# Audio tower on one core: two key blocks read in 64-row matmuls, one expert between the reads, moves on two queues

## The chip, the cores and the metric

The kernel runs on one core of a Trainium2 chip. The time is the device time of one execution in microseconds; lower is better. TensorE is called PE here, VectorE DVE, ScalarE ACT, GpSimd POOL and SyncE SP, as in the profile.

## What is computed

All arithmetic is in fp32. 64 audio signals of 80,000 samples are padded and cut into 157 frames of 512, and each frame goes through a 512-point cosine transform: `h` of 64 x 157 x 512. Then come an attention layer without a softmax and a layer with 16 experts, each behind a layer norm and with a residual.

```python
key_phase = jnp.tanh(x @ Wk + bk) * pi          # 4 sets of 8 planes
query_phase = jnp.tanh(x @ Wq + bq) * pi
V = x @ Wv + bv
for s in range(N_SETS):                          # causal: cumsum over time
    bound = key_ph[:, :, s, :, None] * V[:, :, None, :]
    memory = jnp.cumsum(bound, axis=1)
    retrieved = (memory * jnp.conj(qry_ph[:, :, s, :, None])).sum(axis=2).real
    total = total + weights[s] * retrieved
...                                              # the same once more with fixed phases of the position
total = gate * total + (1.0 - gate) * pos_contrib
return x + total / norm @ Wo + bo
...
scores = softmax(mean(x, axis=1) @ Wg + bg);  idx = argmax(scores)
y = einsum('bsd,bdo->bso', x, We[idx]) + be[idx];  out = scores[idx] * y
```

The running sums are written as a masked product: every query sums the values of all keys not later than itself, weighted with the cosine of the phase difference.

## The kernel before

The 64 examples are worked in 16 groups of 4 (`GB`). A group's tokens are cut into 5 blocks of 32 per example: tile `n` holds one block of each of the 4 examples, 4 x 32 = 128 rows. Tiles 0 to 3 and `TAIL` = 4 hold the time blocks 1, 2, 3, 0 and 4 (`BLOCK`); in the free axis tokens stand in the order `SLOT`.

The order of the work is written out by hand, function by function, and each engine runs its own instructions in that order. Group `g` goes through these stages; the experts of group `g - 1` and the cosine transform of group `g + 1` are set in between:

- `project_and_values(g)`: key and query projections (L600), the values by seven half-size products in place of eight (`value_product`, L445) and the tail's values by a plain product (L250). The values of tiles 0 to 3 lie in two buffers of tag `v`, the tail's in one of tag `v_t`. In between, the normalized tokens of `g - 1` are transposed in blocks of 32x32 by DVE (`turn_blocks`, L780) into a buffer with the tag `gT`. `move_blocks` (L782 to L790) issues 16 DMAs on SP that move them between partitions into `x2T`, which the experts read. After it `route` and `pick` choose each example's expert, and `fetch` (L890) gathers four weight matrices by indirect DMA from POOL.
- `gate(g)`: seven gate products (`gate_product`, L655), whose first copy out of PSUM (L462) writes a new buffer of tag `gT`, so it waits until the moves have read the old one. After the product with `i == 5`, `scores(g)` (L674 to L683) makes the weights `att` of all key blocks: per tile and example a matmul of keys by queries, 32 columns of the array each, into one bank, then two DVE operations. `SEES` says which slots of the queries a key tile is seen by; all tiles side by side are `NS` = 480 columns, with the mask `hmask`.
- `experts_and_embedding(g)`: the experts of `g - 1` for the tail and for tiles 0 and 1 (`expert`, L936, sets of four matmuls that take 32 columns of the array each), the transform of `g + 1` (L270, L272) and its statistics; ACT copies its results out of PSUM (L292, L293) and, after POOL's deviations, scales the residuals (L323).
- `attention(g)`: `read(g, c)` for the four chunks `c` of 128 output features. A read is 20 matmuls of 32 rows (L697): for each key tile one per example, from the array's four row groups into four banks, with 320, 256, 192, 128 and 64 columns for the tiles 3, 0, 1, 2 and `TAIL` (half for the learned phases, half for the fixed ones). A bank pair is one PSUM buffer, and there are four of these; a read takes two. DVE combines each read with the gate in four operations (L705). Then the expert of tile 2 of `g - 1`, and the output products (`output_product`, L445, and the tail's L250), with the expert of tile 3 inside.

Groups 0 and 15 have no expert of an older group between or behind the reads. Group 0 has its own beginning (`first_values`, `first_gate`), and after group 15 come the last experts.

Of the kernel before, what the change touches and what calls it, by code (L numbers as in the profile page):

```python
# [14 lines left out]
F32 = mybir.dt.float32  # L15
# [5 lines left out]
B, L, D = 64, 157, 512  # L21
T_IN = 80000
P = 128
C = D // P
H = D // 2
GB = 4
NG = B // GB
LP = 160
Q = P // GB
NM = LP // Q  # L30
TAIL = NM - 1
SLOT = [0, 1, 3, 4, 2]
# [6 lines left out]
E = 16  # L39
# [3 lines left out]

SEES = [(0, 4 * Q), (Q, 4 * Q), (2 * Q, 4 * Q), (0, LP), (2 * Q, 3 * Q)]
START = [sum(hi - lo for lo, hi in SEES[:n]) for n in range(NM)]
NS = sum(hi - lo for lo, hi in SEES)

# [4 lines left out]
def audio_tower(ctx: ExitStack, tc: tile.TileContext, a, out):  # L54
# [420 lines left out]
    def value_buffer(g, n):  # L475

        s = S[g]
        if n == TAIL:
            s["v", n] = p1.tile([P, D], F32, tag="v_t", name="v_t")
        else:  # L480
            s["v2", n // 2] = v = p1.tile([P, 2, D], F32, tag="v", name="v", bufs=2)
            for b in range(2):
                s["v", n + b] = v[:, b, :]
# [19 lines left out]
    def keep_product(g):  # L503

        s = S[g]
        i, ps = s.pop("ps")
        if i == 1:
            value_buffer(g, 0)
            value_buffer(g, 2)
        gather(i, ps, [[s["v2", m][:, :, n : n + H] for n in (0, H)] for m in range(2)])  # L510

    def add_bv(g, m, of=slice(0, D)):
        v = S[g]["v2", m][:, :, of]
# [17 lines left out]
    def constants():  # L531


        nc.vector.tensor_scalar(hbg, hbg, 0.5, None, ALU.mult)

        sw = lambda name, n: small.tile([2 * F, n], F32, tag=name, name=name, bufs=1)
        mx, ex, sm, rs, pk = sw("sw1", 1), sw("sw2", SETS), sw("sw3", 1), sw("sw4", 1), sw("sw5", 1)
        nc.vector.tensor_reduce(mx, setw, AX.X, ALU.max)
        nc.vector.tensor_scalar(ex, setw, mx, None, ALU.subtract)
        nc.scalar.activation(ex, ex, AF.Exp)  # L540

        nc.scalar.activation(sigp, posw, AF.Tanh, scale=0.5)

        turns = p2.tile([2 * PLANES, LP], F32, tag="even", name="turns")
        nc.vector.tensor_scalar(turns, pos, freqs, None, ALU.mult)
        for _ in range(2):
            whole = p2.tile([2 * PLANES, LP], F32, tag="be", name="whole", bufs=1)
            nc.vector.tensor_scalar(whole, turns, ROUND, ROUND, ALU.add, ALU.subtract)
            rest = p2.tile([2 * PLANES, LP], F32, tag="even", name="rest")
            nc.vector.tensor_tensor(rest, turns, whole, ALU.subtract)  # L550
            turns = rest
        folded = p2.tile([2 * PLANES, LP], F32, tag="be", name="folded", bufs=1)
        nc.vector.scalar_tensor_tensor(folded, turns, ptrig[:, 0:1], turns, ALU.mult, ALU.max)
        nc.scalar.activation(pf, folded.rearrange("p (s t) -> p s t", t=Q), AF.Sin, bias=ptrig[:, 2:3], scale=ptrig[:, 1:2])
        nc.gpsimd.memset(kf[2 * F :], 0.0)
        nc.gpsimd.memset(qf[2 * F :], 0.0)
        yield
        nc.vector.tensor_reduce(sm, ex, AX.X, ALU.add)
        nc.vector.reciprocal(rs, sm)
        nc.vector.tensor_tensor(ex, ex, setsel, ALU.mult)  # L560
        nc.vector.tensor_reduce(pk, ex, AX.X, ALU.add)
        nc.vector.tensor_tensor(wvec, pk, rs, ALU.mult)
        nc.vector.tensor_scalar(sigp2, sigp, 1.0, None, ALU.add)
        nc.vector.tensor_scalar(sigp, sigp, 0.5, 0.5, ALU.mult, ALU.add)
        yield
        ps = bank()
        for n in range(NM):
            lo, hi = SEES[n]
            for i in range(GB):
                to = ps[Q * i : Q * (i + 1), START[n] : START[n] + hi - lo]  # L570
                nc.tensor.matmul(to, pf[:, SLOT[n]], pf[:, lo // Q : hi // Q], start=True, stop=True)
        nc.vector.scalar_tensor_tensor(share, ps[:, :NS], sigp2, hmask, ALU.mult, ALU.mult)
        yield
        rows = slice(2 * F, 2 * F + 2 * PLANES)
        for i in range(GB):
            nc.gpsimd.tensor_copy(kf[rows, :, i], pf)
            nc.vector.tensor_scalar(qf[rows, :, i], pf, sigp[: 2 * PLANES], -1.0, ALU.mult, ALU.mult)
        yield
# [95 lines left out]
    def scores(g):  # L674

        ps = bank()
        for n in range(NM):
            lo, hi = SEES[n]
            for i in range(GB):
                to = ps[Q * i : Q * (i + 1), START[n] : START[n] + hi - lo]  # L680
                nc.tensor.matmul(to, kf[:, SLOT[n], i], qf[:, lo // Q : hi // Q, i], start=True, stop=True)  # L681
        nc.vector.tensor_tensor(att[:, 0], ps[:, :NS], hmask, ALU.mult)
        nc.vector.tensor_tensor(att[:, 1], att[:, 0], share, ALU.add)  # L683

    def read(g, c):

        s = S[g]
        parts = [psum(), psum()]
        banks = [ps[:, b, : 2 * LP] for ps in parts for b in range(2)]

        for n in (3, 0, 1, 2, TAIL):
            for i in range(GB):
                q = slice(Q * i, Q * (i + 1))
                lo, hi = SEES[n]
                to = banks[i].rearrange("p (s t) -> p s t", s=2)[:, :, lo:hi]
                by = att[q, :, START[n] : START[n] + hi - lo]
                nc.tensor.matmul(  # L697
                    to, s["v", n][q, c * P : (c + 1) * P], by, start=(n == 3), stop=(n == TAIL)
                )
        for k, ps in enumerate(parts):  # L700
            of = slice(2 * k, 2 * k + 2)
            r = ps[:, :, : 2 * LP].rearrange("p b (s n t) -> p b s n t", s=2, n=NM)
            th = s["gT"][:, c].rearrange("p (n b t) -> p b n t", n=NM, b=GB)[:, of]
            for n, op in enumerate((ALU.mult, ALU.add)):
                nc.vector.tensor_tensor(th, r[:, :, n], th, op)  # L705
# [76 lines left out]
    def move_blocks(g):  # L782

        s = S[g]
        x = p1.tile([P, GB, C, LP], F32, tag="x2T", name="x2T")
        of = s["blocks2"].rearrange("p (q c) t -> p q c t", c=C)
        for b in range(GB):
            for q in range(GB):
                nc.sync.dma_start(out=x[Q * q : Q * (q + 1), b], in_=of[Q * b : Q * (b + 1), q])  # L789
        s["x2T"] = x.rearrange("p b c t -> p c b t")  # L790

    def turn_x2(g, n, copy=nc.scalar.copy):
        s = S[g]
# [20 lines left out]
    def route_own(g):  # L814

        s = S[g]
        late, total = s.pop("late"), s.pop("early")
        add(total, total, late)
        part = p2.tile([P, E, C * GB], F32, tag="u", name="part")
        nc.vector.tensor_tensor(part, rwq, total.unsqueeze(1).to_broadcast([P, E, C * GB]), ALU.mult)  # L820
        each = p2.tile([P, E], F32, tag="each", name="each")
        nc.vector.tensor_reduce(each, part, AX.X, ALU.add)
        own = p2.tile([P, GB, E], F32, tag="own", name="own")
        nc.vector.tensor_tensor(own, quad, each.unsqueeze(1).to_broadcast([P, GB, E]), ALU.mult)
        s["own"] = own.rearrange("p b e -> p (b e)")

# [34 lines left out]
    def pick(g):  # L861
# [5 lines left out]
        s["top"] = top = t("top", [P, GB])  # L867
        nc.vector.tensor_reduce(top, logit, AX.X, ALU.max)

        score = t("score", wide)  # L870
        nc.vector.tensor_tensor(score, logit, over(top), ALU.is_equal)
        nc.vector.tensor_tensor(score, score, revexp, ALU.mult)
        s["rev"] = rev = t("rev", [P, GB])
# [172 lines left out]
    def first_gate():  # L1046
# [13 lines left out]
        scores(0)  # L1060
        embed(1, 2)
        embed_statistics(1, 2)
        for n in (1, 2, 3, TAIL):
            add_bo(0, n)
        weights()
# [15 lines left out]
    def project_and_values(g):  # L1081
# [16 lines left out]
        turn_blocks(g - 1, 0)  # L1098
        keep_value(g, TAIL)
        turn_blocks(g - 1, 1)  # L1100
        move_blocks(g - 1)
        S[g - 1]["late"] = xsum(g - 1, 2 * Q, L)
        value_product(g, 2)
        keep_product(g)
        add_bv(g, 0, slice(0, H))
        phasors(g)
        value_product(g, 6)
        keep_product(g)
# [18 lines left out]
    def gate(g):  # L1127
        ahead = g + 1 < NG
        for i in (1, 6, 2, 7, 5, 4, 3):
            gate_product(g, i)  # L1130
            if i == 1:
# [2 lines left out]
                fold_once(g + 1, 1)  # L1134
                add_bv(g, 0, slice(H, D))
                add_bv(g, 1)
            elif i == 5:
                scores(g)
                fold_twice(g + 1, 1)
                if ahead:  # L1140
# [8 lines left out]
    def experts_and_embedding(g):  # L1149
# [3 lines left out]
        for n in (2, 3, TAIL):  # L1153
            embed(new, n)
            embed_statistics(new, n)
        embed_deviations(new)
        load_half(g + 2, 0)
        load_half(g + 2, 1)
# [9 lines left out]
    def attention(g):  # L1168
# [6 lines left out]
                pass  # L1175
        for c in range(C):
            read(g, c)
        if ahead and g > 0:
            expert(g - 1, 2)
        S[g]["blocks"] = halves(S[g]["gT"])  # L1180
        made = token_sums(g, tail=False)
        if g == 0:
# [93 lines left out]
def _constants():  # L1276
# [15 lines left out]
    def trig(half, n, turn):  # L1292
# [6 lines left out]
    norm = 1.0 / np.sqrt(np.float64(PLANES) * (at + 1))  # L1299
    causal = (np.arange(LP)[:, None] <= at[None, :]) * norm[None, :] * (at < L)[None, :]  # L1300
    causal[L:] = 0.0
    masks = [causal[Q * BLOCK[n] : Q * (BLOCK[n] + 1), lo:hi] for n, (lo, hi) in enumerate(SEES)]
    setsel = np.tile(np.repeat(np.eye(SETS), PLANES, axis=0), (2, 1))
    f = lambda x: np.ascontiguousarray(x, dtype=np.float32)

# [7 lines left out]
        "lift": f(np.concatenate([np.tan(angle), -np.sin(angle) * np.cos(angle)], axis=1)),  # L1313
        "ptrig": trig(PLANES, 1, 2 * PI),
        "pos": f(np.tile(at, (2 * PLANES, 1))),
        "hmask": f(0.5 * np.tile(np.concatenate(masks, axis=1), (GB, 1))),
        "setsel": f(setsel),
        "quad": f(np.repeat(np.kron(np.eye(GB), np.ones((Q, 1)))[:, :, None], E, axis=2)),
        "revexp": f(np.tile(E - np.arange(E), (P, GB, 1))),
# [65 lines left out]
```

## Time and profile before

| What | Value |
|---|---|
| median of 3 runs | 1331.53 us (1330.65 to 1331.94) |
| the profiled execution, its own time | 1333.84 us |
| its span, first to last instruction | 1332.0 us |
| granted TensorE clock over the span | 1.000 |
| busy: PE, DVE, POOL, ACT | 99%, 78%, 42%, 30% |
| the reads' matmuls, L697 | 2560 records, a group's four reads 7.82 us |
| DVE behind the reads, L705 | 256 operations, 116.7 us, 487 ns each |
| SP's moves into x2T, L789 | 240 issues, median 589 ns each |

An fp32 matmul has two records, so a read of 20 matmuls has 40. The ends of matmuls are modelled, and matmuls of different row or column groups overlap; a stretch of PE is therefore best measured from its start to the start of the next stretch. In the timeline a row is a run of instructions of one line, engine and tile, with start, length, what, and in brackets the engine's idle time before it and what ended that; a line that is called the chain gives start, length and what. In the table of waits a line gives who waited for whom, total us, how often, and the longest.

### The profile page before, as it was taken

How to read it: one execution, taken by the hardware profiler on the slowest of the kernel's cores; microseconds unless marked ns; L12 is line 12 of the kernel's file. 1: busy time of each engine (PE TensorE's matmuls, PEld its weight loads, DVE VectorE, ACT ScalarE, POOL GpSimd, SP SyncE). 2: the span in 40 equal slices, each digit the busy share in tenths (PEclk: the TensorE clock that was granted, in tenths of full speed). 3: DMA queues.
4: the chain of work that ended last, by engine and by line, in shares of the span. 5: the costliest groups of instructions: out<-in, count | busy, mean ns of one | idle time of the engine just before them, and what ended most of it. 6: DMA issues, size and time to landing. Idle time of an engine off the chain costs nothing.

```text
span 1332.0 us, 25132 instructions
## 1 busy us (share of the span) xinstructions
PE 1322.8 (99%) x9784; PEld 871.4 (65%) x9784; DVE 1038.9 (78%) x2074; ACT 403.1 (30%) x708; POOL 556.4 (42%) x658
## 2 busy tenths in 40 slices
PE   9999999999999999999999999999999999999998
PEld 6677666675766667576676666757666675766762
DVE  6888788787777878878787787878878788777583
ACT  2524233141333314233142331413333142341410
POOL 2355344344433355244443443344334542444214
PEclk9999999999999999999999999999999999999999
DMA  7015225052341524315153250524415252241506
GB/s 236 1 51 174 82 58 195 19 176 80 115 140 33 177 70 162 93 45 192 35 175 82 69 183 20 177 79 120 136 36 170 74 171 85 46 152 34 177 8 206
DMA packets 62014, 144.40 MB, mean 108 GB/s; under 512 B 14136, under 2 KB 31432, under 8 KB 53960
## 3 DMA queue, kind: packets, MB, share of 16 engines
q1 hardware_dynamic: 49940, 70.06, 19.9%
q0 software_dynamic: 11456, 72.10, 14.1%
q8 instruction: 78, 1.28, 0.4%
q10 hardware_dynamic: 500, 0.64, 0.2%
q14 instruction: 40, 0.33, 0.1%
HBM read 102.47 MB, written 20.62 MB: 92 GB/s over the span
## 4 chain that ended last, share of the span: by engine, by line
PE 94%; SPq 3%; DMA 1%; issue 1%; POOL 1%; ACT 0%; DVE 0%; ACTq 0%; POOLq 0%
PE mm L445 26%; PE mm L936 20%; PE mm L655 16%; PE mm L697 9%; PE mm L250 9%; PE mm L270 3%; SPq L789 3%; PE mm L600 3%; PE mm L272 3%; PE mm L636 1%; PE mm L681 1%; PE mm L201 1%; DMA x2T<-turned 1%; DMA t_v<-in_we,rows 1%; PE mm L219 0%
## 5 line engine op out<-in xcount | busy, mean ns | idle before, releaser
L936 PE MATMUL mm<-we,x2T 128*32 128x512 f32 x2400 | 270.5, 595 | 0.0
L936 PEld LDWEIGHTS mm<-we,x2T 128*32 128x32 f32 x2400 | 74.2, 110 | 156.0 <-issue 149.5
L705 DVE TENSOR_TENSOR gT<-mm,gT 128x320 f32<-128x320 f32 x256 | 116.7, 487 | 23.4 <-PE mm L697 18.9
L697 PE MATMUL mm<-att,v 32*128 32x256 f32 (+3 forms) x2048 | 123.5, 359 | 0.0
L697 PEld LDWEIGHTS mm<-att,v 32*128 32x128 f32 x2048 | 105.0, 185 | 22.3 <-POOL shift L243 6.7
L237 POOL TENSOR_SCALAR rstd<-mv 128x2 f32<-128x2 f32 (+1 forms) x50 | 11.8, 236 | 245.0 <-DVE mv L233 244.9
L237 POOL TENSOR_SCALAR dev<-mv 128x5 f32<-128x5 f32 (+1 forms) x20 | 10.5, 525 | 234.1 <-DVE mv L233 233.5
L771 ACT ACTIVATE x<-res,shift,rstd 128x512 f32<-128x512 f32 x61 | 46.4, 807 | 202.7 <-POOL shift L244 190.8
L515 POOL TENSOR_TENSOR v<-v,bv 128x512 f32<-128x512 f32 (+1 forms) x45 | 72.9, 1635 | 71.0 <-ACT v L464 71.0
L672 ACT ACTIVATE gT<-gT,hbg 128x320 f32<-128x320 f32 x90 | 45.7, 554 | 166.6 <-DVE gT L100 166.6
L947 DVE SCALAR_TENSOR_TENSOR res<-mm,gate,res 128x512 f32<-128x512 f32 x64 | 47.9, 748 | 56.6 <-PE mm L936 56.5
L232 DVE BATCH_NORM_STATS2 st<-res 128x6 f32<-128x512 f32 x128 | 87.8, 686 | 3.3
L890 POOL DMA_INDIRECT we<-in_we,rows x60 | 69.1, 1151 | 44.4 <-issue 33.4
L327 POOL TENSOR_TENSOR res<-res,bo 128x512 f32<-128x512 f32 x64 | 80.3, 1285 | 13.1 <-ACT res L323 13.0
L445 PE MATMUL mm<-t_o,sum 128*128 128x256 f32 x384 | 85.5, 379 | 0.0
L122 POOL TENSOR_TENSOR xT<-xT 128x640 f32<-128x640 f32 x30 | 46.4, 1546 | 88.6 <-DVE even L100 87.3
L445 PE MATMUL mm<-t_v,sum 128*128 128x256 f32 x360 | 80.1, 379 | 0.0
L445 PEld LDWEIGHTS mm<-t_o,sum 128*128 128x128 f32 x384 | 73.0, 190 | 9.9
L323 ACT ACTIVATE res<-res,shift,more 128x512 f32<-128x512 f32 x64 | 46.9, 803 | 91.8 <-POOL more L313 91.8
L445 PEld LDWEIGHTS mm<-t_v,sum 128*128 128x128 f32 x360 | 68.4, 190 | 9.3
L655 PE MATMUL mm<-xT,wg 128*128 128x320 f32 x240 | 70.0, 434 | 3.2 <-ACT gT L462 3.2
L250 PE MATMUL mm<-wv,xT 128*128 128x512 f32 x160 | 71.8, 592 | 0.0
(218 smaller groups left out, 2789.3 us busy)
## 6 DMA issues: line engine op xcount, KB each, us to landing
xT<-in_frames SPq DMA_DIRECT2D x32, 640.0 KB
x2T<-turned SPq DMA_DIRECT2D x240, 80.0 KB
out<-res SPq DMA_DIRECT2D x236, 64.0 KB
scale<-row SPq DMA_DIRECT2D x15, 320.0 KB
out<-res_t SPq DMA_DIRECT2D x62, 32.0 KB
out<-res_t SPq DMA_DIRECT2D x62, 26.0 KB
wg<-in_wg SPq DMA_DIRECT2D x1, 1024.0 KB
wo<-in_wo SPq DMA_DIRECT2D x1, 1024.0 KB
```

Of the source, the lines that this page charges most:

```text
L232: nc.vector.bn_stats(st, h)
L250: nc.tensor.matmul(ps, tile_of(x[:, c], n), w[:, c, :], start=(c == 0), stop=(c == C - 1))
L323: nc.scalar.activation(s["res"][n], s["res"][n], AF.Identity, bias=shift, scale=more)
L327: nc.gpsimd.tensor_tensor(r, r, bo, ALU.add)
L445: nc.tensor.matmul(ps[:, b, :], lhs[:, c, P * b : P * (b + 1)], w[:, c, :], start=(first and c == 0), stop=(c == 1), skip_group_check=not ...
L515: nc.gpsimd.tensor_tensor(v, v, by, ALU.add)
L655: nc.tensor.matmul(ps[:, o, :HN], w[:, c, o * P : (o + 1) * P], rhs[:, c], start=(first and c == 0), stop=(c == 1), skip_group_check=not f ...
L697: nc.tensor.matmul(to, s["v", n][q, c * P : (c + 1) * P], by, start=(n == 3), stop=(n == TAIL))
L705: nc.vector.tensor_tensor(th, r[:, :, n], th, op)
L890: nc.gpsimd.indirect_dma_start(out=ws[b][:, n * k : n * (k + 1)], out_offset=None, in_=of, in_offset=bass.IndirectOffsetOnAxis(ap=rows[:, ...
L936: nc.tensor.matmul(ps[Q * i : Q * (i + 1), :], s["x2T"][:, c, i, Q * n : Q * (n + 1)], s["ws"][i][:, c, :], start=(c == 0), stop=(c == C - 1),
L947: nc.vector.scalar_tensor_tensor(o, ps, s["gate"], o, ALU.mult, ALU.add)
```

## The change

There are four parts.

1. The key tiles 2 and `TAIL` are read in matmuls of 64 rows. For that the keys of the two tiles are dealt out anew by example (`KEYS`): tile 2's values now hold the blocks 3 and 4 of the examples 0 and 3, those of the tail the blocks of 1 and 2, so that rows 0 to 63 and 64 to 127 are each one example. The tail's scores are made for 64 columns, as wide as tile 2's: `NS` is 512. Where four quadrants had been right already two stay: ACT makes six copies of 32 rows x 512 per group, two in `tail_values` and four in `pair_values`. The tail's values are first written to a buffer of tag `u`, and the exchanged ones stand in `v_t`.
2. In a read the tiles 3, 0, 1 ("single", 32 rows) and 2, `TAIL` ("paired") change their order from chunk to chunk: single, paired, paired, single, single, paired, paired, single.
3. The expert of tile 2 of `g - 1` moves from behind the four reads to between the second and the third (groups 1 to 14).
4. `move_blocks` issues ten moves on SP; the other six are issued on POOL's queue after the first `add_bv`.

Beside these, `own` and `score` have one buffer each instead of two. In groups 1 to 14 `tail_values` stands after the gate product with `i == 2` and `pair_values` behind the embedding's statistics; in group 15 `pair_values` stands ahead of `scores`, and in group 0 both stand in `first_gate`. On PE a group has 16 read matmuls per chunk instead of 20.

```diff
-SEES = [(0, 4 * Q), (Q, 4 * Q), (2 * Q, 4 * Q), (0, LP), (2 * Q, 3 * Q)]
+SEES = [(0, 4 * Q), (Q, 4 * Q), (2 * Q, 4 * Q), (0, LP), (2 * Q, 4 * Q)]
+KEYS = [[(n, i) for i in range(GB)] for n in range(NM)]
+KEYS[2] = [(2, 0), (TAIL, 0), (TAIL, 3), (2, 3)]
+KEYS[TAIL] = [(TAIL, 1), (2, 1), (2, 2), (TAIL, 2)]
...
-            s["v", n] = p1.tile([P, D], F32, tag="v_t", name="v_t")
+            s["v", n] = p2.tile([P, D], F32, tag="u", name="tail")
...
+    def place(g, x, n, of):
+        for q, (m, i) in enumerate(KEYS[n]):
+            if m == of and (x is not S[g]["v", m] or q != i):
+                nc.scalar.copy(x[Q * q : Q * (q + 1)], S[g]["v", m][Q * i : Q * (i + 1)])
+
+    def tail_values(g):
+        S[g]["pair"] = x = p1.tile([P, D], F32, tag="v_t", name="v_t")
+        place(g, x, TAIL, TAIL)
+
+    def pair_values(g):
+
+        s = S[g]
+        x = s.pop("pair")
+        place(g, x, TAIL, 2)
+        place(g, s["v", 2], 2, TAIL)
+        s["v", TAIL] = x
...
-            for i in range(GB):
-                to = ps[Q * i : Q * (i + 1), START[n] : START[n] + hi - lo]
-                nc.tensor.matmul(to, kf[:, SLOT[n], i], qf[:, lo // Q : hi // Q, i], start=True, stop=True)
+            for q, (m, i) in enumerate(KEYS[n]):
+                to = ps[Q * q : Q * (q + 1), START[n] : START[n] + hi - lo]
+                nc.tensor.matmul(to, kf[:, SLOT[m], i], qf[:, lo // Q : hi // Q, i], start=True, stop=True)
...
-        for n in (3, 0, 1, 2, TAIL):
-            for i in range(GB):
-                q = slice(Q * i, Q * (i + 1))
+        single, paired = (3, 0, 1), (2, TAIL)
+        order = (*single, *paired) if c % 2 == 0 else (*paired, *single)
+        seen = set()
+        for n in order:
+            w = Q if n in single else 2 * Q
+            for q in range(0, P, w):
+                i = KEYS[n][q // Q][1]
                 lo, hi = SEES[n]
                 to = banks[i].rearrange("p (s t) -> p s t", s=2)[:, :, lo:hi]
-                by = att[q, :, START[n] : START[n] + hi - lo]
+                by = att[q : q + w, :, START[n] : START[n] + hi - lo]
+                first = i not in seen
+                seen.add(i)
                 nc.tensor.matmul(
-                    to, s["v", n][q, c * P : (c + 1) * P], by, start=(n == 3), stop=(n == TAIL)
+                    to,
+                    s["v", n][q : q + w, c * P : (c + 1) * P],
+                    by,
+                    start=first,
+                    stop=n == (single if c % 2 else order)[-1] or (c % 2 == 0 and n == 2 and i in (0, 3)),
+                    skip_group_check=True,
                 )
...
-        for b in range(GB):
-            for q in range(GB):
-                nc.sync.dma_start(out=x[Q * q : Q * (q + 1), b], in_=of[Q * b : Q * (b + 1), q])
+        moves = [(b, q) for b in range(GB) for q in range(GB)]
+        for k, (b, q) in enumerate(moves):
+            if k == 10:
+                yield
+            queue = nc.sync if k < 10 else nc.gpsimd
+            queue.dma_start(out=x[Q * q : Q * (q + 1), b], in_=of[Q * b : Q * (b + 1), q])
...
-        move_blocks(g - 1)
+        moves = move_blocks(g - 1)
+        next(moves)
         S[g - 1]["late"] = xsum(g - 1, 2 * Q, L)
         value_product(g, 2)
         keep_product(g)
         add_bv(g, 0, slice(0, H))
+        next(moves)
...
         for c in range(C):
             read(g, c)
-        if ahead and g > 0:
-            expert(g - 1, 2)
+            if c == 1 and ahead and g > 0:
+                expert(g - 1, 2)
```

More of the change, by code (lines that the diff above doesn't have):

```diff
@@ L568, in constants @@
             lo, hi = SEES[n]
-            for i in range(GB):
-                to = ps[Q * i : Q * (i + 1), START[n] : START[n] + hi - lo]
-                nc.tensor.matmul(to, pf[:, SLOT[n]], pf[:, lo // Q : hi // Q], start=True, stop=True)
+            for q, (m, _) in enumerate(KEYS[n]):
+                to = ps[Q * q : Q * (q + 1), START[n] : START[n] + hi - lo]
+                nc.tensor.matmul(to, pf[:, SLOT[m]], pf[:, lo // Q : hi // Q], start=True, stop=True)
         nc.vector.scalar_tensor_tensor(share, ps[:, :NS], sigp2, hmask, ALU.mult, ALU.mult)
@@ L678, in scores @@
             lo, hi = SEES[n]
-            for i in range(GB):
-                to = ps[Q * i : Q * (i + 1), START[n] : START[n] + hi - lo]
-                nc.tensor.matmul(to, kf[:, SLOT[n], i], qf[:, lo // Q : hi // Q, i], start=True, stop=True)
+            for q, (m, i) in enumerate(KEYS[n]):
+                to = ps[Q * q : Q * (q + 1), START[n] : START[n] + hi - lo]
+                nc.tensor.matmul(to, kf[:, SLOT[m], i], qf[:, lo // Q : hi // Q, i], start=True, stop=True)
         nc.vector.tensor_tensor(att[:, 0], ps[:, :NS], hmask, ALU.mult)
@@ L689, in read @@
         banks = [ps[:, b, : 2 * LP] for ps in parts for b in range(2)]
-        for n in (3, 0, 1, 2, TAIL):
-            for i in range(GB):
-                q = slice(Q * i, Q * (i + 1))
+        single, paired = (3, 0, 1), (2, TAIL)
[5 more added lines that the diff above has]
+                i = KEYS[n][q // Q][1]
                 lo, hi = SEES[n]
                 to = banks[i].rearrange("p (s t) -> p s t", s=2)[:, :, lo:hi]
-                by = att[q, :, START[n] : START[n] + hi - lo]
+                by = att[q : q + w, :, START[n] : START[n] + hi - lo]
+                first = i not in seen
+                seen.add(i)
                 nc.tensor.matmul(
-                    to, s["v", n][q, c * P : (c + 1) * P], by, start=(n == 3), stop=(n == TAIL)
+                    to,
[4 more added lines that the diff above has]
+                    skip_group_check=True,
                 )
@@ L786, in move_blocks @@
         of = s["blocks2"].rearrange("p (q c) t -> p q c t", c=C)
-        for b in range(GB):
-            for q in range(GB):
-                nc.sync.dma_start(out=x[Q * q : Q * (q + 1), b], in_=of[Q * b : Q * (b + 1), q])
+        moves = [(b, q) for b in range(GB) for q in range(GB)]
[4 more added lines that the diff above has]
+            queue.dma_start(out=x[Q * q : Q * (q + 1), b], in_=of[Q * b : Q * (b + 1), q])
         s["x2T"] = x.rearrange("p b c t -> p c b t")
+        yield
     def turn_x2(g, n, copy=nc.scalar.copy):
@@ L822, in route_own @@
         nc.vector.tensor_reduce(each, part, AX.X, ALU.add)
-        own = p2.tile([P, GB, E], F32, tag="own", name="own")
+        own = p2.tile([P, GB, E], F32, tag="own", name="own", bufs=1)
         nc.vector.tensor_tensor(own, quad, each.unsqueeze(1).to_broadcast([P, GB, E]), ALU.mult)
@@ L868, in pick @@
         nc.vector.tensor_reduce(top, logit, AX.X, ALU.max)
-        score = t("score", wide)
+        score = p2.tile(wide, F32, tag="score", name="score", bufs=1)
         nc.vector.tensor_tensor(score, logit, over(top), ALU.is_equal)
@@ L1062, in first_gate @@
         embed_statistics(1, 2)
+        tail_values(0)
+        pair_values(0)
         for n in (1, 2, 3, TAIL):
@@ L1136, in gate @@
                 add_bv(g, 1)
+            elif i == 2:
+                tail_values(g)
             elif i == 5:
+                if not ahead:
+                    pair_values(g)
                 scores(g)
@@ L1155, in experts_and_embedding @@
             embed_statistics(new, n)
+        pair_values(g)
         embed_deviations(new)
@@ L1301, in _constants @@
     causal[L:] = 0.0
-    masks = [causal[Q * BLOCK[n] : Q * (BLOCK[n] + 1), lo:hi] for n, (lo, hi) in enumerate(SEES)]
+    masks = [
+        np.concatenate([causal[Q * BLOCK[m] : Q * (BLOCK[m] + 1), lo:hi] for m, _ in KEYS[n]])
+        for n, (lo, hi) in enumerate(SEES)
+    ]
     setsel = np.tile(np.repeat(np.eye(SETS), PLANES, axis=0), (2, 1))
@@ L1315, in _constants @@
         "pos": f(np.tile(at, (2 * PLANES, 1))),
-        "hmask": f(0.5 * np.tile(np.concatenate(masks, axis=1), (GB, 1))),
+        "hmask": f(0.5 * np.concatenate(masks, axis=1)),
         "setsel": f(setsel),
```

## The prediction

> **What bounds the kernel now.** I read the page's busy times first, then the chain that ended last.
>
> ```profile
> PE 1322.8 (99%) x9784; PEld 871.4 (65%) x9784; DVE 1038.9 (78%) x2074; ACT 403.1 (30%) x708; POOL 556.4 (42%) x658
> ...
> PE 94%; SPq 3%; DMA 1%; issue 1%; POOL 1%; ACT 0%; DVE 0%; ACTq 0%; POOLq 0%
> ```
>
> TensorE is the bound: 99% busy, 94% of the chain. So an edit is worth what it does to the spacing of matmuls. The same chain in order of time (start, length, what) gives prices. One group:
>
> ```profile
> 703.40 7.00 PE mm L936 x64
> 710.40 7.82 PE mm L697 x145
> 718.22 3.57 PE mm L936 x32
> 723.72 3.43 PE mm L250 x8
> 727.15 6.91 PE mm L445 x32
> 734.05 3.57 PE mm L936 x32
> 737.63 3.65 PE mm L445 x16
> ```
>
> Each fp32 matmul is two records, two passes over its columns; the four 32-column expert matmuls of a set run together. L936: 16 sets take 7.00 and 8 take 3.57, so a set pass of 512 columns costs 0.429 us and a stretch pays 0.14 once. L445: 32 passes of 256 columns in 6.91 are 0.216 each; the 16 at 737.63, which stand between stretches of other array shapes, take 3.65, or 0.19 more than 16 x 0.216. **Every change of the array's shape costs about 0.2 us.** PE's own timeline (start, length) puts it in place:
>
> ```profile
> 710.33 1.80 PE L697 MATMUL mm<-att,v 32*128 32x320 f32 x32
> ...
> 712.12 1.75 PE L697 MATMUL mm<-att,v 32*128 32x320 f32 x32
> ...
> 713.87 1.96 PE L697 MATMUL mm<-att,v 32*128 32x320 f32 x26
> ...
> 718.15 3.64 PE L936 MATMUL mm<-we,x2T 128*32 128x512 f32 x32
> 721.72 1.99 PE L445 MATMUL mm<-wo,gT 128*128 128x256 f32 x8
> 723.55 3.60 PE L250 MATMUL mm<-wo,gT 128*128 128x512 f32 x8
> ```
>
> From 721.72 to 723.55 is 1.83 for 8 passes of 0.216: 0.10 extra on entry, where the second weight load isn't hidden. The expert from 718.15 to 721.72 is 0.14 over 8 x 0.429: 0.03 for its entry (32 columns to load) and 0.11 for the way out. So a stretch with 128 weight columns costs 0.10 + 0.11 = **0.21**.
>
> The first read starts at 710.33, the second at 712.12, the third at 713.87: 1.79, 1.75. All four take 7.82 to 718.15; at 1.75 they would take 1.79 + 3 x 1.75 + 0.1 for the way out = 7.14. The missing 0.7 is VectorE:
>
> ```profile
> 712.34 3.78 DVE L705 TENSOR_TENSOR gT<-mm,gT 128x320 f32<-128x320 f32 x8 [1.11 <-PE mm L697]
> 716.28 3.79 DVE L705 TENSOR_TENSOR gT<-mm,gT 128x320 f32<-128x320 f32 x8 [0.16 <-PE mm L697]
> ```
>
> It empties a read in 3.78/2 = 1.89 us, more than 1.75, and there are four PSUM buffers with two per read; the third and fourth reads wait for them.
>
> **Reads as pairs.** By columns, at 0.833 ns a column and pass and 2.5 ns a pass (from 0.216 and 0.429), four row tiles together: blocks of 320, 256, 192, 128 and 64 columns are 2 x (0.269 + 0.216 + 0.163 + 0.109 + 0.056) = 1.63. Measured is 1.75; the 64-column tail can't hide its 128-column loads. After, the three single blocks are 1.295 and the two 64-row pairs, now both 128 columns wide, 4 passes of 0.109 = 0.436 if the two halves run together: 1.73. So pairing saves nearly nothing, and it adds shape changes: order is single, paired, paired, single, expert, single, paired, paired, single.
>
> No row shows a 64-row tile or a step from 32 rows to 64. Lower bound: free. Upper bound: a full change, 0.21. I take 0.21, since every change of shape in this trace pays it, also the one from 128 to 64 columns (L445 to L600: eight sets at 0.269 are 2.15; that stretch takes 2.30 in the chain). The Trainium skill, "TensorEngine Tiling (Array Packing)", section Key Properties, speaks against this edit: a change of tiling mode, unlike one of tile, drains the engine, and it lists 32x128 and 64x128 as different modes; no run here shows that pair. By the rule the sum below is 1335, by the bare column count 1322 to 1324.
>
> **Expert 2 between reads.** With 3.57 us of expert after read 1, VectorE has emptied reads 0 and 1 before read 2 needs their buffers, so the 0.7 stall goes. What is late next is VectorE's read 3: PE ends read 3 as the output products begin, VectorE starts 0.25 later, as now, and takes 1.89, so it ends about 2.1 us into them, where it now has an expert to catch up. Its sums, the scaling (2.88) and the tail's addition then come 1.2 us later, but it idles 0.16, 0.97 and 1.03 just after, waiting for PE L445, so product 7 finds it on time.
>
> Sum for groups 1 to 14, from the first read to the output products. Before: 7.82 + 3.57 = 11.39. After: four single stretches 5.18, pairs 1.74, expert 3.57, six stretches x 0.21 = 1.26: 11.76. So **+0.37, x14 = +5.2**. Groups 0 and 15 have no expert there: 5.18 + 1.74 + five stretches x 0.21 + some 0.25 still waiting for VectorE = 8.2 against 7.82: **+0.8** for both.
>
> **Scores.** Last block 64 columns, not 32: two passes x 32 x 0.833 ns x 16 = **+0.85** on PE. VectorE's two operations on it grow from 480 to 512 columns (0.66 and 1.28 by 7%): 0.13 us, needed by the reads 18 us later. Nothing.
>
> **Exchange of values.** Six copies of 32x512 on ScalarE per group. Nearest rows: 128x129 in 0.27, 128x512 in 0.59; at 0.59, 57 us in all, a seventh of ScalarE's time. Two stand in a 4.28 us wait for gT's additions, four in a 6.26 us wait for POOL's `more` (L313); they end some 4 us before the first pair. Group 0 has six in a gap of 3.47: 0.1 over, at most. Without this cover they would cost up to 3.5 us a group. The tail's values take a turn in tag u's two buffers: four allocations a group instead of three, each released long before. Smaller buffers of `own` and `score`: one use a group. Nothing.
>
> **Moves.** Now SP issues 16 in a row, and the gate's first copy out of PSUM waits for the last to read gT's buffer (SP's timeline, ACT's, and the sums of waits):
>
> ```profile
> 750.35 11.30 SPq L789 DMA_DIRECT2D x2T<-turned  x16
> ```
>
> ```profile
> 763.29 0.69 ACT L462 COPY gT<-mm 128x640 f32<-128x640 f32 x1 [6.50 <-DMA x2T<-turned]
> ```
>
> ```profile
> PE mm L655 <- ACT gT L462: 3.2, 4, 2.2
> ```
>
> SP issues one per 0.63. PE pays only where the moves are late: from the starts of its gate products the gaps are 0.64, 0.38, 0.54 and 2.35 over the usual 2.15 in groups 4, 9, 14 and 15, and 0.1 each for the weight load after them: 4.3. After, ten issues end near 756.8. The last six go to POOL after `add_bv`, which ends at 752.64, before `fold_once` at 758.25, a wait of 5.61. POOL's direct DMA rows show 0.51 an issue; with 0.30 between, 4.9, landing 3.3 later: about 761, before the gate product ends at 761.5. Behind them stand `fold_once` and the weights' indirect DMAs (1.66 us of slack, then landing 8.8 after issue, about 775.7, for an expert at 777.95). If a move took as long as an indirect one, 1.15, POOL would be 3 us late and the 2.2 us of slack would take most of it. I take **-4.3**; the other end is 0.
>
> Sum: 5.2 + 0.8 + 0.85 - 4.3 = **+2.6** against the profiled execution: 1333.84 us, of which 1332.0 is span, so 1336.4. The median shown is 1331.53, 2.3 below that execution. If those 2.3 lie outside the steps above, the result is 1334.1; if the median runs have less of the late moves, only 2.0 can be won there and it is 1336.4. I take the middle, **1335.3**, own range 1332 to 1338.
>
> **Rivals.**
> - *The step from 32 to 64 rows is free, or half price.* For it: the weights have 128 columns in both shapes, and the four row groups already run apart (the third read's two halves drift while one waits). Against: all shape changes in the trace pay. Free: 4 x 0.21 less in each of 14 groups is 11.8, groups 0 and 15 at zero; sum -6.5 + 0.85 - 4.3 = -10: 1322 to 1324. Half: -3.7: 1328 to 1330. This is the other side: below 0.12 per step, the change is faster by over 0.2%.
> - *The moves don't pay.* POOL issues or lands late, and PE waits as now or longer: 4.3 to 6 more, 1339 to 1341. Against: POOL's 5.61 us gap.
> - *Two 64-row halves don't run together.* Pairs double: 0.436 x 64 reads = 28 more, 1363. Against: two 64-column tiles of L600 run as one set.
>
> **Numbers.** Forecast 0.55, free or half-price step 0.25 (about half each), moves without gain 0.13, halves in turn 0.05, other 0.02. The range takes in the free step and the moves' loss, 1322 to 1341; it leaves out the 0.05 and edges. About 0.2%, 2.7 us, is what a measurement of this kernel can tell from no change: 1328.8 to 1334.2. Faster: free 0.13, part of half 0.07, other 0.02: 0.22. Same: rest of half 0.05, forecast's lower end 0.18: 0.23. Slower: 0.55.
>
> **What would show it.** Right: two reads with the pairs between them take about 4.0 from the first single to the expert or product; VectorE's additions no longer hold L697; the L697 pairs run in sets of two, 0.109 apart, with about 0.1 before and 0.1 after the first pass; ScalarE's first gate copy no longer waits for x2T. Wrong: a pair that follows a single at the usual spacing (1322), sets of one (1363), or a wait for the moves that is still there.

## The result and the profile after

| | before | changed |
|---|---|---|
| median | 1331.76 us of 15 runs (1329.67 to 1336.28) | 1337.38 us of 15 runs (1336.69 to 1338.46) |
| ratio | | 1.0042, 95% interval 1.0034 to 1.005 |
| profiled execution: own time, span | 1333.84, 1332.0 | 1337.48, 1335.5 |

The changed kernel is slower by 0.42%, 5.6 us; 1335.3 with a range of 1322 to 1341 was forecast. TensorE is still the bound, and SP, which issues the moves, has left the chain (3% before):

```profile
PE 1327.9 (99%) x9272; PEld 857.7 (64%) x9272; DVE 1032.1 (77%) x2074; ACT 465.6 (35%) x804; POOL 594.3 (44%) x748
...
PE 97%; issue 1%; DMA 1%; POOL 1%; SPq 0%; DVE 0%; POOLq 0%
```

PE has 512 records fewer and is busy for longer. The chain in order of time (start, length, what) for one group, the changed lines against the fence in the prediction:

```profile
706.89 7.00 PE mm L971 x64
713.89 4.11 PE mm L723 x64
718.00 3.57 PE mm L971 x32
721.57 4.11 PE mm L723 x64
725.68 1.92 PE mm L448 x8
...
737.94 3.57 PE mm L971 x32
741.51 3.65 PE mm L448 x16
```

(L971, L723 and L448 are the lines that were L936, L697 and L445.) Everything but the reads has its old price: 7.00, 3.57, 3.65. Two reads now take 4.11; four took 7.82 with VectorE's hold in them. Inside a pair of reads PE's timeline (start, length, what) shows why:

```profile
713.82 2.00 PE L723 MATMUL mm<-att,v 32*128 32x320 f32 x28
715.65 0.39 PE L723 MATMUL mm<-att,v_t 64*128 64x128 f32 x4
715.88 0.39 PE L723 MATMUL mm<-att,v 64*128 64x128 f32 x4
716.10 0.39 PE L723 MATMUL mm<-att,v_t 64*128 64x128 f32 x4
716.42 1.58 PE L723 MATMUL mm<-att,v 32*128 32x320 f32 x24
717.93 3.64 PE L971 MATMUL mm<-we,x2T 128*32 128x512 f32 x32
...
721.50 2.00 PE L723 MATMUL mm<-att,v 32*128 32x320 f32 x28
...
725.61 0.70 PE L448 MATMUL mm<-wo,gT 128*128 128x256 f32 x2
```

In the rows of 28 and of 24 records the first 24 are the 32-row blocks; the last four of a row of 28 are the first 64-row pair, whose weights lie in the same tile. The four records of a pair, two passes of two matmuls, follow each other at 0.22, so a 128-column pass takes 0.11 and the two halves run together, as the sum assumed. But from 713.82, through 1.295 of single blocks, eight pair passes of 0.11 (0.89) and the 0.10 that the first stretch pays behind its first pass, the next single should start at 716.11; it starts at 716.42, 0.31 later. The starts of single matmuls in the trace place the rest: the last pass of a single block is followed 0.27 later (its columns take 0.16), the first pair pass 0.21 later (columns 0.11), the last pair pass 0.21 later, and the next single's first pass 0.37 later (columns 0.27). So each step has about 0.1 before the first pass of the new shape and 0.10 behind it. Three of these four parts make the 0.31; the fourth, 0.10, lies behind 716.42.

VectorE, which held the reads back, no longer does. Its idle time before the second row was 0.16; now it waits for PE both times:

```profile
716.07 3.90 DVE L736 TENSOR_TENSOR gT<-mm,gT 128x320 f32<-128x320 f32 x8 [1.36 <-PE mm L723]
...
723.75 3.90 DVE L736 TENSOR_TENSOR gT<-mm,gT 128x320 f32<-128x320 f32 x8 [1.36 <-PE mm L723]
```

The moves do what was meant. SP's timeline, POOL's, and ScalarE's sums of waits (us, times, longest):

```profile
754.24 6.28 SPq L823 DMA_DIRECT2D x2T<-turned  x10
```

```profile
756.47 3.14 POOL L823 DMA_DIRECT2D x2T<-turned  x6
762.14 1.54 POOL L125 TENSOR_TENSOR xT<-xT 128x640 f32<-128x640 f32 x1 [2.54 <-DVE even L103]
```

```profile
ACT gT L465 <- PE mm L675: 73.8, 15, 4.9
```

POOL's six issues end 2.5 us before it is needed again, and the gate's first copy waits for its product in all 15 groups, no longer for `x2T`. So each group is alike: from first read to first read it takes 81.04 us thirteen times over (632.78 to 713.82 in the timeline is one). Before, the same period was 80.59 where no move was late (629.74 to 710.33 is one), and up to 81.33 where one was.

### The profile page after: what moved, and what is told of

Same layout as the page of the kernel before. It is cut to its first block, busy times and chain, and to the rows that moved or that the text cites. A ratio compares the mean times of both kernels' runs of the same rounds, so it can differ in the third digit from the quotient of the medians.

```text
span 1335.5 us, 24297 instructions
## 1 busy us (share of the span) xinstructions
PE 1327.9 (99%) x9272; PEld 857.7 (64%) x9272; DVE 1032.1 (77%) x2074; ACT 465.6 (35%) x804; POOL 594.3 (44%) x748
## 4 chain that ended last, share of the span: by engine, by line
PE 97%; issue 1%; DMA 1%; POOL 1%; SPq 0%; DVE 0%; POOLq 0%
PE mm L448 29%; PE mm L971 19%; PE mm L675 17%; PE mm L723 10%; PE mm L253 9%; PE mm L273 3%; PE mm L620 3%; PE mm L275 3%; PE mm L656 1%; PE mm L701 1%; DMA t_v<-in_we,rows 1%; DMA tables<-in_table_sums 0%; PE mm L204 0%; PE mm L222 0%; PE mm L866 0%
## 5 line engine op out<-in xcount | busy, mean ns | idle before, releaser
L971 PE MATMUL mm<-we,x2T 128*32 128x512 f32 x2400 | 269.9, 595 | 0.0
L971 PEld LDWEIGHTS mm<-we,x2T 128*32 128x32 f32 x2400 | 72.0, 110 | 159.9 <-issue 154.2
L736 DVE TENSOR_TENSOR gT<-mm,gT 128x320 f32<-128x320 f32 x256 | 119.8, 489 | 45.8 <-PE mm L723 40.8
L723 PE MATMUL mm<-att,v 32*128 32x320 f32 (+3 forms) x1792 | 127.3, 378 | 0.0
L723 PEld LDWEIGHTS mm<-att,v 32*128 32x128 f32 (+1 forms) x1792 | 92.8, 184 | 45.1 <-issue 19.6
L448 PE MATMUL mm<-t_o,sum 128*128 128x256 f32 x384 | 85.5, 379 | 0.0
L448 PE MATMUL mm<-t_v,sum 128*128 128x256 f32 x360 | 80.1, 379 | 0.0
L448 PEld LDWEIGHTS mm<-t_o,sum 128*128 128x128 f32 x384 | 73.0, 190 | 9.9
L925 POOL DMA_INDIRECT we<-in_we,rows x60 | 60.4, 1007 | 34.3 <-DVE rows L921 20.3
L448 PEld LDWEIGHTS mm<-t_v,sum 128*128 128x128 f32 x360 | 68.4, 190 | 9.3
L103 DVE TENSOR_TENSOR res<-mm,res 128x512 f32<-128x512 f32 x64 | 43.4, 678 | 33.8 <-PE mm L448 17.4
L675 PE MATMUL mm<-sum,wg 128*128 128x320 f32 x240 | 69.5, 432 | 0.0
```

The lines of the kernel that those rows point to most:

```text
L448: nc.tensor.matmul(ps[:, b, :], lhs[:, c, P * b : P * (b + 1)], w[:, c, :], start=(first and c == 0), stop=(c == 1), skip_group_check=not ...
L675: nc.tensor.matmul(ps[:, o, :HN], w[:, c, o * P : (o + 1) * P], rhs[:, c], start=(first and c == 0), stop=(c == 1), skip_group_check=not f ...
L723: nc.tensor.matmul(to, s["v", n][q : q + w, c * P : (c + 1) * P], by, start=first, stop=n == (single if c % 2 else order)[-1] or (c % 2 == ...
L925: nc.gpsimd.indirect_dma_start(out=ws[b][:, n * k : n * (k + 1)], out_offset=None, in_=of, in_offset=bass.IndirectOffsetOnAxis(ap=rows[:, ...
L971: nc.tensor.matmul(ps[Q * i : Q * (i + 1), :], s["x2T"][:, c, i, Q * n : Q * (n + 1)], s["ws"][i][:, c, :], start=(c == 0), stop=(c == C - 1),
```

## The experiments

Medians are set against the runs of before on the same chip: 1331.94 (27 runs) for the first four, 1331.07 (12 runs) for the others. The ratios on record are not quotients of these medians; in the first four, where the runs of before reach up to 1341.30, they lie at or below them. The changed kernel's 1337.38 belongs to the 15 runs of the result, with 1331.76 for before. "Period" is the time from a group's first read to the next group's, from PE's starts. My theory: the change consists of two gains, VectorE's hold and the late moves, and one loss, four changes of array shape per group at 0.21. The rivals: the loss comes from the expert's new place, from POOL's queue, from the wider tail, or from the copies.

**The moves alone** (`e1_moves`): before, with the fourth part of the change, shortened here; the six moves on POOL stand behind the first `add_bv`.

```diff
-                nc.sync.dma_start(out=x[...], in_=of[...])
+            queue = nc.sync if k < 10 else nc.gpsimd
+            queue.dma_start(out=x[...], in_=of[...])
```

> The kernel before with the moves alone changed (ten on SP, six on POOL after the first add_bv). Theory: PE's waits for late moves go and nothing else changes; the profiled execution of before held 4.4 us of them, and its own time lay 2.1 above the median, so the gain in the median is 2 to 4 us: 1328 to 1330. In the profile ScalarE's first gate copy waits for PE L655 and no longer for x2T, and the period of a group, from first read to first read, is 80.6 in all of the groups 1 to 14. Rival, that POOL's issues or the landing of its DMAs cost what SP saves: 1331.8 or more, and the copy still waits for x2T.

Measured: 1330.41 us, ratio 0.9982 (0.9967 to 0.9997). The period is 80.59 or 80.60 in every group, and ScalarE's line is the changed kernel's:

```profile
ACT gT L462 <- PE mm L655: 73.7, 15, 4.9
```

The mechanism is right. The gain in the median is 1.5 us, short of the 2 to 4 expected; by the means of all runs it is 2.5 (1333.04 to 1330.49). The highest run is 1331.70 of 11, against 1341.30 of 27 before; only one execution of each has a trace, so what held the slowest ones is not shown.

**The expert alone** (`e2_expert`).

```diff
             read(g, c)
-        if ahead and g > 0:
-            expert(g - 1, 2)
+            if c == 1 and ahead and g > 0:
+                expert(g - 1, 2)
```

> The kernel before with the expert of tile 2 alone moved between the second and the third read. Theory: VectorE no longer holds up the third and fourth reads: two reads 3.64, expert 3.57, two reads 3.64 make 10.85 in place of 11.39, 0.54 in each of 14 groups, 7.6 us: 1324. Rival, that the later end of VectorE's additions delays the output products or the layer norm behind them: same time or slower, with a wait of PE L445 for DVE.

Measured: 1324.33 us, ratio 0.9943 (0.9926 to 0.996). The period is 80.05 where no move is late, 0.54 under 80.59, as worked out. The rival is out: no wait of L445's matmuls for DVE is in the sums, and its weight loads wait for DVE as in before (6.9 us in 14 groups), and 0.8 once more.

**Both, without pairs** (`e3_both`): the edits of `e1_moves` and `e2_expert` together.

> The changed kernel without its pairs and their copies: the kernel before with the expert between the reads and the moves on two queues. Theory, that the pairs' changes of array shape are all that the change loses: e1 and e2 add up, 1320 to 1323, some 15 us below the changed kernel (11.78 - 10.85 + 0.05 for the scores is 0.98 in each of 14 groups, about 0.6 in groups 0 and 15). Rival, that the loss comes from the expert's place or from POOL's queue: over 1331.

Measured: 1323.03 us, ratio 0.9925 (0.9897 to 0.9953): 8.9 us under before and 14.3 under the changed kernel's median, at the upper edge of what was expected. The period is 80.05 or 80.06 throughout. The chain:

```profile
699.27 7.00 PE mm L940 x64
706.28 3.64 PE mm L697 x80
709.92 3.57 PE mm L940 x32
713.49 3.64 PE mm L697 x80
```

Two reads with the expert behind them take 3.64, as worked out for `e2_expert`, against 4.11 with pairs. VectorE's timeline shows that the later end of its additions is made up, as the prediction said:

```profile
723.86 0.68 DVE L100 TENSOR_TENSOR res_t<-mm,res_t 128x512 f32<-128x512 f32 x1
...
725.99 0.68 DVE L100 TENSOR_TENSOR u<-mm,u 128x512 f32<-128x512 f32 x1
727.70 0.69 DVE L100 TENSOR_TENSOR u<-mm,u 128x512 f32<-128x512 f32 x1 [1.03 <-PE mm L445]
```

The output products begin at 717.06 here, and at 721.72 in before. The tail's addition comes 6.80 after that (5.47 in before), the first addition to `u` 8.93 after (8.92 in before), and the next one waits 1.03 for PE, as in before.

**One queue again** (`e4_one_queue`): the changed kernel with one line replaced.

```diff
-            queue = nc.sync if k < 10 else nc.gpsimd
+            queue = nc.sync
```

> The changed kernel with all 16 moves on SP again (the last six stay behind the first add_bv in the program, which is another engine, so SP issues them in a row). Theory: 2 to 4 us slower than the changed kernel, 1339 to 1341, some groups with PE waiting for ScalarE's first gate copy, which waits for x2T; the groups without such a wait have the changed kernel's period of 81.04. Rival, that the two queues gain nothing in ordinary executions: 1337.4.

Measured: 1339.15 us, ratio to before 1.005 (1.0032 to 1.0069), 1.8 over the changed kernel's median. Seven of its 13 periods lie above 81.04, up to 81.76, and ScalarE waits for the moves again:

```profile
ACT gT L465 <- DMA x2T<-turned: 66.4, 12, 6.7
```

With 1.5 in `e1_moves` and 1.3 between `e2_expert` and `e3_both` the moves are worth 1.3 to 1.8 us by the medians, 2.2 to 2.5 by the means. Each of the three differences alone is little more than the runs spread by; together with the waits that go and come back they agree.

**Another order** (`e5_order`): the changed kernel, with the same order in every chunk and the stop flags to match.

```diff
-        order = (*single, *paired) if c % 2 == 0 else (*paired, *single)
+        order = (*single, *paired)
...
-                    stop=n == (single if c % 2 else order)[-1] or (c % 2 == 0 and n == 2 and i in (0, 3)),
+                    stop=n == order[-1] or (n == 2 and i in (0, 3)),
```

> The changed kernel with the order single, paired in every chunk, so that a group has eight stretches of reads instead of six. Theory, that each change of array shape costs 0.21: 0.42 in each of 14 groups, period 81.46 in place of 81.04, and three stretches more in groups 0 and 15, less what VectorE's wait took there: 6.5 us over the changed kernel, 1343 to 1345. Rival, that the pairs cost by themselves, whatever their order: 1337.4.

Measured: 1343.78 us, ratio to before 1.0095 (1.0076 to 1.0114), 6.4 over the changed kernel. The period is 81.43 or 81.44, where 81.46 was worked out. The same matmuls in another order cost 0.20 more for each change of shape added, one in every two reads (4.31 against 4.11 in the chain):

```profile
709.09 7.00 PE mm L971 x64
716.09 4.31 PE mm L723 x64
720.40 3.57 PE mm L971 x32
723.97 4.31 PE mm L723 x64
```

So the loss isn't a price that the pairs have whatever their order, as the rival said. What is left for such a price is told by `e7_wide`.

**Pairs alone** (`e6_pairs`): the changed kernel with its expert behind the reads and all moves on SP, by undoing the edits of `e1_moves` and `e2_expert`.

> The kernel before with the pairs alone (exchanged values, wider tail scores, alternating order); expert behind the reads, all moves on SP. Theory: all groups read as group 0 of the changed kernel does, 8.44 instead of 7.82, and 0.05 for the scores: 0.67 x 16 = 10.7 us over before, 1342 to 1343. Rival, that VectorE's pace hides the changes of shape here, since it holds back the reads anyway by 0.7: 1333.

Measured: 1343.59 us, ratio 1.0094 (1.0075 to 1.0114). The chain has the four reads of every group at group 0's price:

```profile
708.58 7.00 PE mm L967 x64
715.58 8.44 PE mm L723 x126
724.01 3.57 PE mm L967 x32
```

8.44 is 0.62 over 7.82, and the period, 81.26 where no move is late, is 0.67 over 80.59, as worked out: 10.7 in 16 groups. The median is 12.5 over its before and 0.6 above the range expected; the further 1.8 are not accounted for by this execution, whose own time is 1341.83. Single blocks (5.18), pairs (16 passes of 0.11, 1.78) and five stretches at 0.21 make 8.0, which by subtraction leaves VectorE some 0.45 where it held the reads by 0.7 before. So it hides a quarter of a microsecond of the steps and not the 0.7 of the rival.

**The same columns in 32 rows** (`e7_wide`): `e3_both` with the tail as wide as in the changed kernel.

```diff
-SEES = [(0, 4 * Q), (Q, 4 * Q), (2 * Q, 4 * Q), (0, LP), (2 * Q, 3 * Q)]
+SEES = [(0, 4 * Q), (Q, 4 * Q), (2 * Q, 4 * Q), (0, LP), (2 * Q, 4 * Q)]
```

> The version with the expert between the reads and the moves on two queues, 32-row reads throughout, with the tail's scores and reads 64 columns wide as in the changed kernel: the same columns through the array, no 64-row matmul, no exchange. Theory: a read takes 5 blocks of 1.735 in place of 1.75, the scores 0.05 more: 1323 to 1325, 13 to 14 us below the changed kernel, which then is the price of the changes of shape alone. Rival, that the wider tail costs part of the loss: up to 4 passes x 0.05 x 64 = 7 us more, 1330.

Measured: 1324.98 us, ratio 0.9949 (0.9935 to 0.9964). The period is 80.21 or 80.22, 0.16 over `e3_both`: two wider reads are 3.69 instead of 3.64, twice, and the scores the rest. The expectation had a read of 1.735 for one of 1.75, so no difference to speak of. A read does take 1.74 here; but of the 1.75 in `e3_both` 0.05 is a delay that the 64-column tail of the read before puts on the first pass, and the first read of each two has none: there one read costs 1.75 and the other 1.69.

```profile
701.57 7.00 PE mm L940 x64
708.57 3.69 PE mm L697 x80
712.26 3.57 PE mm L940 x32
715.83 3.69 PE mm L697 x80
```

This is the closest relative of the changed kernel: as many columns through the array, all in tiles of 32 rows. It lacks the 64-row matmuls and the copies. Its pair of reads takes 3.69, the changed kernel's 4.11: 0.42 for two changes of shape, 0.21 each. The period differs by 81.04 - 80.21 = 0.83, four of them. Four at the 0.20 of `e5_order` are 0.80, so about 0.03 a group is left for the pairs themselves, the copies and the smaller buffers.

**Copies twice** (`e8_copies`): the changed kernel, with each copy made twice in all groups but the first.

```diff
-                nc.scalar.copy(x[...], S[g]["v", m][...])
+                for _ in range(2 if g else 1):
+                    nc.scalar.copy(x[...], S[g]["v", m][...])
```

> The changed kernel with each of ScalarE's six copies made twice in the groups 1 to 15. Theory: copies of 0.63 us stand in ScalarE's idle time, 2.5 of 4.3 us behind the second gate product and 5.0 of 6.1 ahead of the residuals, so doubled they cost nothing in groups 1 to 14 and below 2 us in group 15, where the last two gate activations stand behind them: 1337 to 1339. Rival, that they are on the path: 3.8 us x 15, 1394, or a part of it.

Measured: 1337.24 us, ratio to before 1.0045 (1.0029 to 1.0061), the period 81.04 as before the doubling. ScalarE's timeline shows the gap nearly filled, and the tile `more`, which POOL makes and the residuals wait for, still comes later:

```profile
787.88 2.54 ACT L519 COPY v_t<-v 32x512 f32<-32x512 f32 x4
790.43 2.55 ACT L519 COPY v<-tail 32x512 f32<-32x512 f32 x4
793.96 2.93 ACT L326 ACTIVATE res<-res,shift,more 128x512 f32<-128x512 f32 x4 [0.97 <-POOL more L316]
```

The copies are free where they stand; the four of `pair_values` have about 1 us to spare at double their number.

## Why the prediction came out as it did

- *The forecast as a whole* was right in its direction and its mechanism, and short in size. Slower was forecast at 0.55, by 3.8 us over the 1331.53 then known; it is 5.6 over 1331.76, still inside the likeliest case's own range of 1332 to 1338.
- *The step from 32 to 64 rows* was the open cost, bounded by 0 and 0.21 and taken at 0.21. It is 0.21 (`e7_wide`), and 0.20 for each one more (`e5_order`). The rival that it is free or half price is shown wrong. "TensorEngine Tiling (Array Packing)" in the Trainium skill, section Key Properties, says that a change of tiling mode drains the engine, and gives no price. The about 0.1 ahead of the first pass of each new shape agrees with that; no row shows the drain itself. The prediction's sentence that no row shows a 64-row tile is not right: at L355, in the set-up, the trace of before has two transposes of 64 rows, which start together (39.410 and 39.413), and the 128-column pass of 128 rows ahead of them is followed 0.20 later, not 0.11. So a change of rows from 128 to 64 had a price of 0.09 on its way in, and two 64-row halves ran together, before anything was tried.
- *The halves run together*: right, passes of 0.11; the rival of 1363 is out.
- *Expert between the reads*: right. 0.54 a group was in the sum, 0.54 is measured, and VectorE's later end takes up its waits of 0.16 and 0.97 for PE, while the third, 1.03, stays.
- *Groups 1 to 14*: +0.37 and 0.05 for the scores were worked out, the period shows 81.04 - 80.59 = 0.45, so 0.03 more a group.
- *Groups 0 and 15*: mis-sized. 8.2 was taken for the four reads, 8.44 is measured in group 0 (8.51 in group 15, where before has 7.88): by the sum above VectorE holds two of them back by some 0.45 and not 0.25. +1.2 for both instead of +0.8.
- *Copies, smaller buffers, scores*: no cost beyond the 0.05. `e8_copies` shows the copies' cover; no run takes the smaller buffers apart, but `e7_wide` leaves about 0.03 a group for them.
- *The moves* are the term that was furthest off: -4.3 by the profiled execution, -2.0 as the other reading, and -1.3 to -1.8 by the medians of three pairs of kernels (-2.2 to -2.5 by their means). The waits go as said; the execution shown was one of the worse ones (1333.84 against a median of 1331.76), and 2.35 of the 4.3 stood in one group. The page of one execution gave the size of a wait that differs from execution to execution. Even for that one it was short: by the periods, the late moves add up to 5.0, since those of four more groups cost 0.15 to 0.23 each.
- *The sum between the two profiled executions* was met by luck. From group 0's first read to the end of group 15's reads it is 1199.20 before (71.64 to 1270.84) and 1201.75 changed (72.62 to 1274.37): +2.55, where the sum says +2.6. But the reads and scores cost 7.5, where 6.85 was taken, and the moves gave 5.0, where 4.3 was taken; the two misses cancel.

With the measured terms: 14 x 0.45 = 6.3, 0.67 each for groups 0 and 15 makes 7.6, less 1.5 for the moves: 6.1, against 5.6 measured. The rest is below what the medians tell apart.

**So where did the gains go?** They are there, and worth 8.9 us together (`e3_both`); the pairs cost 14 and bring nothing. Four 32-row tiles, which start within 0.02 us of each other, already cover all 128 rows. Two 64-row matmuls take the place of four, but a pass of 128 columns takes 0.11 us in either shape, and there are as many passes.

## What to carry to other kernels

Count the sets of matmuls that run together, price each by its columns, and add the changes of array shape: 0.2 us each here for fp32 weights of 128 columns, more than a whole 128-column pass. Here merging small tiles removed matmuls but no set, and so gained nothing. A stall that one profile shows in some groups and not in others is a draw, not a mean: price it by executions, not by the one that was traced; and try the parts of a bundled change apart, since here two of the three were worth keeping.

## What the runs showed of the hardware

- The price of a change of shape had two halves at the reads, the pairs, the experts and the output products: about 0.10 to 0.12 before the first matmul of the new shape, and behind it 0.10 for 128 weight columns, 0.03 for 32 (the expert). The second half reads as a weight load that isn't hidden: in the changed kernel the second pair's load starts at 715.436, 0.11 after the first's, and its matmul at 715.542. A change of the row count alone, with the same 128 columns, pays both.
- A 128-column pass of a 32-row and of a 64-row tile takes the same 0.11 us (`e7_wide` and the changed kernel). The two 64-column passes of the 32-row tail took 0.17 together, where the columns alone say 0.11, and the first pass of a read behind them came 0.05 later (0.325 in place of 0.272); the loads of their 128 weight columns are the likely reason. Widening the tail from 64 to 128 columns cost only 0.05 for two reads, a quarter of what the columns alone say.
- POOL issued a direct DMA of 80 KB every 0.52 us, SP one every 0.63 (six in 3.14, ten in 6.28); POOL's landed 2.9 after issue, in the median.
